# Attention's PSUM banks in three kinds, its fourth head apart, and DVE's part of each task one round later

## The chip, the cores and the metric

The kernel runs on one core of one Trainium2 chip. Its time is the device time of one launch, in microseconds (us); shorter is better. In the profile the engines are PE (TensorE: matmuls and transposes through an identity), PEld (PE's weight loads), DVE (VectorE), ACT (ScalarE), POOL (GpSimd) and SP (SyncE, which here only issues DMAs). Each engine takes its instructions in the order in which the program lists them; a semaphore makes one wait for another.

## The reference

Two layers, each with adaptive normalisation, an attention and a feed-forward part, over 16 batches (B) of 256 tokens (T) of width 128 (D). The change lies in layer 0's attention, 16 heads of width 8:

```python
h = _layernorm(x, axis=-1) * (1 + ca) + sa          # sa, ca, ga per batch, from silu(c) @ wmod
qkv = h @ Wqkv + bqkv
content = einsum('bhid,bhjd->bhij', q, k)
rel = pad(einsum('bhid,rd->bhir', q, rel_emb), one on the left)[..., :L]
attn = softmax((content + rel) / sqrt(8), axis=-1)
out = einsum('bhij,bhjd->bhid', attn, v)
x = x + ga * (out.reshape(B, L, D) @ Wout + bout)
```

After it come a feed-forward of 16 experts (a router picks 4 of them per token), and layer 1: a cumulative-sum attention with phases, and a gated feed-forward with a time shift. These are in both kernels the same.

## The kernel before

Attention is cut into 64 rounds: 16 batches times NR = 4 rounds of four heads. Two batches make a chunk, eight chunks in all. Round n belongs to batch b = n // 4, r = n % 4.

In a round the four heads g = 0 to 3 lie on 32 partitions each (`rows_ = slice(32 * g, 32 * g + 32)`), so that their matmuls use different rows of PE's array. They go through these steps, spread over rounds:

- `scores(n)` (L446): for each head two matmuls of 32 x 128 x 256 into a bank `s`, 128 x 512. Order: the first half of all four heads, then the second half.
- `row_maxima(n, s)` (L466): DVE takes the negated row maximum of each of the four banks. After an odd round, `maxima` gets the upper bits and (on POOL, L472) the rest.
- `with_maxima(pair)` (L477, L482): every second round DVE transposes the maxima of the two rounds before, and SP moves them into `max_rows` with four DMAs.
- `weights(n)` (L491, L501): LAG = 4 rounds later the transposed scores are computed in banks `st`, starting from the negated maximum (one matmul with `takes`, then two of `kx` by `qx`), and ACT takes their exp (L509) into `exp`.
- `values(n, exp)` (L521): one round after that, 16 PE instructions multiply by `v_aug`, which holds v and a column of ones, into a bank `po`; ACT copies it out (L532, L535), POOL adds (L536).

All eight PSUM banks are one pool, `p_m`. Each tile takes the next bank in turn and waits until the tile that had it eight tiles ago has been read.

Beside the rounds run tasks: Python generators that stop at named places, and go on when the round's loop comes to a place of that name (`take_step`). The places of a round, in order: scores and row maxima, "dve" (statistics of the normalisation, L549, L550), weights, values, "mid" and "end" (PE's part), then the copies that are due, "take" (DVE's part: it reads what "end" left in a bank), one load of later weights, "after", "late" (the router's steps). The tasks are

- `project(c)`: normalises chunk c (POOL scales, L555), transposes it (`pln`, L569), makes q and k (`pq` L627, `pk` L633), splits q and k into upper bits and rest (`halves`: `q_high`, `k_high`, L456, rest by L599) and later v (`pv`, L669). It starts in round 8c-12 for chunk c (chunk 1 in round 0).
- `attn_end(b)`: transposes the output (`pot`, L720), divides by the sums (L724, L726), transposes back (`pu`, L732), multiplies by Wout (`py`, L739), and adds to x (`y`, L742, L743, L744).
- `chunk_end(c)`: the second batch's `attn_end`, then layer 0's second normalisation and the router's logits (`pl`, L750, L754).

The operands of scores need each head's four components (upper bits and rest of q and k in all pairings) on neighbouring partitions. So q and k go through DRAM: `put_aside` writes the upper bits and the rest to `q_halves` and `k_halves` (L647, two pairs of DMAs, one pair per round), and `spread` reads the rows for r = 0 to 3 into `qx` and `kx` (L616, a pair per round). `copies` says in which round each pair is issued. Only batch 0's first round goes directly (`at_once`, L592). The tiles `q_whole`, `k_whole`, `q_high`, `k_high` have one buffer each.

Chunk 0 is made ahead of the rounds by `project_first`, batch 0 and then batch 1, with q's DMAs on ACT's queue and k's on SP's.

## Time and profile before

| | us |
|---|---|
| median of 3 runs | 1077.78 (1077.56 to 1080.33) |
| the profiled execution | 1081.92 |
| its span | 1080.1 |
| first maximum of round 0 | 23.71 |
| of round 8 (chunk 1) | 58.48 |
| of round 16 (chunk 2) | 94.31 |
| of round 63, the last | 295.73 |
| first matmul of the experts | 313.34 |

| engine | busy us | share of the span |
|---|---|---|
| PE | 987.2 | 91% |
| DVE | 831.8 | 77% |
| ACT | 703.2 | 65% |
| POOL | 823.2 | 76% |

The granted clock of TensorE was 0.973 of full speed on the mean. "Busy" counts the time in which an engine has an instruction under way; matmuls are pipelined, so a busy PE need not be full. A row of a view names the line, the engine, the operation, the tile written and the tiles read, and the idle time of the engine just before, with what ended it. The first round's times above are starts of L466 in the timeline. The rounds take some 290 of 1080 us; what follows is bound by PE throughout (27.0 of 27.0 us busy in most stretches from 324 us on).

### The profile page before, as it was taken

To read this page: it belongs to the slowest core of one execution; us is meant where nothing else is said; L and a number is where in the kernel's file an instruction comes from. 1 tells how busy PE (TensorE), PEld (TensorE's weight loads), DVE (VectorE), ACT (ScalarE), POOL (GpSimd) and SP (SyncE) were. 2 spreads that over 40 slices of the span, in tenths; PEclk is the share of its full clock that TensorE was granted. 3 is DMA by queue.
4 is the path that set the end of the run, shared out by engine and by line. 5 is a ranking of instruction groups with operands and counts; after the bars stand their busy time and mean duration, and the time that the engine had idled before them with its cause. 6 is when DMAs were issued, how large, how long until landed. Compare 5 with 4: busy or idle time off the path is not lost. (4 is left out here: it accounts for less than half of the span.)

```text
span 1080.1 us, 14265 instructions
## 1 busy us (share of the span) xinstructions
PE 987.2 (91%) x4529; PEld 483.3 (45%) x4529; DVE 831.8 (77%) x1296; ACT 703.2 (65%) x1490; POOL 823.2 (76%) x807
## 2 busy tenths in 40 slices
PE   5778988889999999999999999898999999999987
PEld 4444555456544444444444434333444444444334
DVE  4858888888835465866556555799999999999995
ACT  2446666666675778787867756365767668768662
POOL 2636556554366777888878788899999999999992
PEclk9989989788999999999999999999999999999999
DMA  5654643233042222223322322200000000000000
GB/s 169 217 180 145 204 153 139 88 120 133 7 151 85 98 98 80 107 90 117 108 89 98 99 87 89 78 10 11 10 10 29 11 20 30 0 10 6 5 10 20
DMA packets 58859, 86.74 MB, mean 80 GB/s; under 512 B 13312, under 2 KB 32288, under 8 KB 58784
## 3 DMA queue, kind: packets, MB, share of 16 engines
q1 hardware_dynamic: 55952, 83.47, 22.8%
q10 hardware_dynamic: 2832, 2.36, 0.7%
q8 instruction: 36, 0.59, 0.2%
q14 instruction: 39, 0.32, 0.1%
HBM read 62.73 MB, written 22.29 MB: 79 GB/s over the span
## 5 line engine op out<-in xcount | busy, mean ns | idle before, releaser
L509 ACT ACTIVATE exp<-st 128x512 f32<-128x512 f32 x256 | 132.2, 603 | 89.9 <-PE st L501 89.8
L466 DVE TENSOR_REDUCE raw<-s 128x2 f32<-128x512 f32 x256 | 160.2, 678 | 20.3 <-PE s L446 20.3
L918 POOL TENSOR_TENSOR u<-u,wide 128x512 f32<-128x512 f32 x128 | 162.8, 1272 | 10.3 <-DVE u L917 0.2
L917 DVE SCALAR_TENSOR_TENSOR u<-pg,u 128x512 f32<-128x512 f32 x128 | 87.7, 686 | 78.8 <-POOL u L911 78.7
L926 PE MATMUL acc<-u,w_dn 128*128 128x512 f32 x256 | 133.7, 604 | 6.3 <-POOL u L918 6.1
L1331 DVE TENSOR_TENSOR_SCAN sum_assoc<-keep,bound_assoc 128x1024 f32<-128x1024 bf16 (+1 forms) x58 | 125.8, 2170 | 9.5 <-POOL bound_assoc L1328 9.5
L903 PE MATMUL pg<-hT,w_gu 128*128 128x512 f32 x256 | 131.2, 594 | 0.4 <-DVE logits L754 0.4
L905 PE MATMUL pup<-hT,w_gu 128*128 128x512 f32 x256 | 130.8, 592 | 0.6 <-ACT u L908 0.6
L911 POOL TENSOR_SCALAR u<-u 128x512 f32<-128x512 f32 x128 | 79.4, 620 | 63.0 <-ACT u L908 55.7
L1328 POOL TENSOR_TENSOR bound_assoc<-v,phasor 128x1024 f32<-128x1024 f32 x57 | 124.7, 2187 | 1.7 <-ACT phasor L1314 1.6
L1549 POOL TENSOR_TENSOR sum_assoc<-sum_assoc,phasor 128x1024 f32<-128x1024 f32 (+1 forms) x58 | 121.5, 2095 | 0.6 <-DVE sum_assoc L1331 0.6
L1331 DVE TENSOR_TENSOR_SCAN mem<-keep,bound_pos 128x1024 f32<-128x1024 bf16 x52 | 118.2, 2272 | 0.0
L906 ACT ACTIVATE pg<-pg,b_gu 128x512 f32<-128x512 f32 x128 | 84.0, 656 | 51.8 <-PE pg L903 51.3
L1328 POOL TENSOR_TENSOR bound_pos<-v,rotor 128x1024 f32<-128x1024 f32 x51 | 111.5, 2186 | 0.0
L1345 PE MATMUL pout<-m_pos,w_pos 128*128 128x512 f32 x204 | 97.2, 599 | 14.2 <-ACT oT L1370 10.7
L1345 PE MATMUL pout<-sum_assoc,w_assoc 128*128 128x512 f32 x228 | 107.6, 594 | 2.0 <-POOL sum_assoc L1549 1.8
L908 ACT ACTIVATE u<-pup,b_gu 128x512 f32<-128x512 f32 x128 | 87.8, 686 | 18.4 <-PE pup L905 16.7
L521 PE MATMUL po<-exp,v_aug 128*32 128x256 f32 x1024 | 80.1, 435 | 10.3 <-DVE raw L466 10.0
L1312 ACT ACTIVATE phasor<-off 128x512 f32<-128x512 f32 x56 | 35.1, 627 | 68.8 <-DVE off L1306 67.5
L926 PEld LDWEIGHTS acc<-u,w_dn 128*128 128x128 f32 x256 | 46.6, 189 | 73.8 <-issue 39.0
L905 PEld LDWEIGHTS pup<-hT,w_gu 128*128 128x128 f32 x256 | 50.2, 196 | 60.5 <-issue 51.2
L491 PE MATMUL st<-max_rows,takes 32*128 32x512 f32 x256 | 58.2, 476 | 14.6 <-DVE heads L726 10.2
(313 smaller groups left out, 1869.6 us busy)
## 6 DMA issues: line engine op xcount, KB each, us to landing
wide<-scores SPq DMA_DIRECT2D x64, 512.0 KB, 3.6
qx<-q_halves SPq DMA_DIRECT2D x28, 256.0 KB, 3.1
kx<-k_halves SPq DMA_DIRECT2D x28, 256.0 KB, 3.0
q_halves<-q_high SPq DMA_DIRECT2D x7, 512.0 KB, 3.1
k_halves<-k_high SPq DMA_DIRECT2D x7, 512.0 KB, 3.7
q_halves<-q_whole SPq DMA_DIRECT2D x7, 512.0 KB, 3.1
k_halves<-k_whole SPq DMA_DIRECT2D x7, 512.0 KB, 4.3
there<-total SPq DMA_DIRECT2D x12, 256.0 KB, 2.1
```

What stands on the lines that cost most here:

```text
L466: nc.vector.tensor_reduce(raw[:, :, g, n % 2], s[g], AX.X, ALU.max, negate=True)
L509: nc.scalar.activation(e[:, g, :, :], st[g], AF.Exp, scale=QSCALE)
L903: nc.tensor.matmul(pg, w_gu[:, e, 0 : 2 * D : 2], h2, start=True, stop=True)
L905: nc.tensor.matmul(pu, w_gu[:, e, 1 : 2 * D : 2], h2, start=True, stop=True)
L908: nc.scalar.activation(u, pu, AF.Identity, bias=b_gu[:, 1, e : e + 1])
L917: nc.vector.scalar_tensor_tensor(u, pg, MOST, u, ALU.min, ALU.mult)
L918: nc.gpsimd.tensor_tensor(u, u, wide[n // SOME][:, n % SOME, :], ALU.mult)
L926: nc.tensor.matmul(accs[c], w_dn[:, e, :], work.pop(n), start=False, stop=(e == NE - 1))
L1328: nc.gpsimd.tensor_tensor(w[nm], v2, bind, ALU.mult)
L1331: nc.vector.tensor_tensor_scan(dst[:, half].rearrange("p s k t -> p (s k t)"), keep.rearrange("p (s k) t -> p s k t", k=2)[:, half].rearra ...
L1345: nc.tensor.matmul(pos[c], w[:, j, :], m[:, k, :, :].rearrange("p k t -> p (k t)"), start=(j == 0 and i == 0 and k == 0), stop=(c < NCH - ...
L1549: nc.gpsimd.tensor_tensor(m[:, part], m[:, part], phasor[(n - 1) % 3][:, part, :, 1:], ALU.mult)
```

## The change

- **Banks.** The eight banks become three pools: three for `s`, three for `st`, two for everything else in the rounds. Ahead of the rounds, `bank` goes round a list of the pools.
- **Fourth heads apart.** A round's PE order becomes: the fourth head's `st` of the round before (weights n-5), `s` of heads 0 to 2, `st` of heads 0 to 2 (weights n-4), `s` of head 3, then values, "mid", "end". With three banks each, `s` of head 3 takes head 0's bank of the same round, and `st` of head 2 takes the bank of the fourth head's `st` just before.
- **"take" moves.** DVE's part of a task no longer ends its round; it runs between the maxima of heads 1 and 2 of the next round. q's upper bits, which were taken at "mid", move there too (ahead of k's). The copies that follow from it are counted from that round, so they leave a round later; the wait before `pv` is one shorter.
- **First batches.** The statistics of batches 0 and 1 are taken one after the other, their projections follow each other, `pv` of both comes last. Only the four direct DMAs of batch 0's q stay on ACT's queue; all other moves and reads of chunk 0 are issued by SP, first the eight moves, then the fourteen reads.

```diff
-            p_m = scope.enter_context(tc.tile_pool(name="pa_m", bufs=8, space=bass.MemoryType.PSUM))
+            p_s, p_st, p_m = (
+                scope.enter_context(tc.tile_pool(name=nm, bufs=n, space=bass.MemoryType.PSUM))
+                for nm, n in (("pa_s", 3), ("pa_st", 3), ("pa_m", 2))
+            )
...
-            home = {"psum": p_m}
+            home = {"psum": [p_s, p_s, p_st, p_st, p_m, p_m, p_s, p_st]}
             def bank(shape, nm):
-                return home["psum"].tile(shape, F32, tag="m", name=nm)
+                homes = home["psum"]
+                homes.append(homes.pop(0))
+                return homes[-1].tile(shape, F32, tag="m", name=nm)
...
-            def scores(n):
+            def scores(n, s, heads):
-                s = [bank([P, NIT, T], f"s_{n}_{g}") for g in range(4)]
+                for g in heads:
+                    s[g] = p_s.tile([P, NIT, T], F32, tag="m", name=f"s_{n}_{g}")
                 for i in range(NIT):
-                    for g in range(4):
+                    for g in heads:
...
                     if g == 0 and n >= 2 and n % 2 == 0:
                         with_maxima(n // 2 - 1)
+                    if g == 1:
+                        take_step("take", True)
...
-            def weights(n):
+            def weights(n, heads):
-                st = [bank([P, NIT, T], f"st_{n}_{g}") for g in range(4)]
+                st = {g: p_st.tile([P, NIT, T], F32, tag="m", name=f"st_{n}_{g}") for g in heads}
...
                 nc.scalar.activation(qf, pq, AF.Identity, bias=bq)
-                q = halves(True, qf, nc.gpsimd)
                 yield "end"
...
                 nc.vector.scalar_tensor_tensor(
                     kf, pk, bk, rel.unsqueeze(1).to_broadcast([P, n, T]), ALU.add, ALU.add
                 )
+                q = halves(True, qf, nc.gpsimd)
                 k = halves(False, kf, nc.gpsimd if c else nc.vector)
...
-                    queue = nc.scalar if of_q and not c else nc.sync
                     if not c and not of.start:
-                        at_once(c, of, of_q, parts, 0, queue)
+                        at_once(c, of, of_q, parts, 0, nc.scalar if of_q else nc.sync)
...
                 if not c:
-                    for each in moves + reads[0 if of.start else 1 :]:
-                        for go in each:
-                            go()
+                    firsts.extend(go for each in moves for go in each)
+                    reads_first.extend(go for each in reads[0 if of.start else 1 :] for go in each)
+                    yield "values"
                 for i, each in enumerate(moves + reads if c else []):
                     copies.setdefault(now[0] + 1 + i, []).extend(each)
-                for i in range(LAG if c > 1 else 0):
+                for i in range(LAG - 1 if c > 1 else 0):
                     yield "after"
...
-            start(project_first(0, hT_first), rank=0)
-            take_step("dve")
-            modulation(0, wmod0, sc0, (0, 1), p_m)
+            batches = [project_first(k, hT_first) for k in range(2)]
+            for k in (0, 0, 0):
+                next(batches[k])
+            modulation(0, wmod0, sc0, (0, 1), p_s)
+            for k in (1, 1):
+                next(batches[k])
...
+            for go in firsts + reads_first:
+                go()
+            for k in range(2):
+                assert next(batches[k], None) is None
...
-                    s = scores(n)
+                if n > LAG:
+                    weights(n - LAG - 1, (3,))
+                s = {}
+                if n < len(rounds):
+                    scores(n, s, (0, 1, 2))
+                if LAG <= n < len(rounds) + LAG:
+                    weights(n - LAG, (0, 1, 2))
+                if n < len(rounds):
+                    scores(n, s, (3,))
                     row_maxima(n, s)
...
-                if LAG <= n < len(rounds) + LAG:
-                    es[n - LAG] = weights(n - LAG)
...
-                take_step("take", True)
```

More of the change, by code (lines that the diff above doesn't have):

```diff
@@ L399, in rest_of_setup @@
             def rest_of_setup():
-                modulation(0, wmod0, sc0, (3, 4, 5), p_m)
+                modulation(0, wmod0, sc0, (3, 4, 5), p_st)
                 pg = bank([B, D], "pgate")
@@ L452, in scores @@
                         )
-                return s
             def upper(out, src):
@@ L482, in with_maxima @@
                     nc.sync.dma_start(rows_[m], turned[32 * m : 32 * m + 16])
-            def weights(n):
+            def weights(n, heads):
                 b, r = rounds[n]
                 c, k = divmod(b, 2)
-                e = ap.tile([P, 4, NIT, T], F32, tag="exp", name=f"exp_{n}")
-                st = [bank([P, NIT, T], f"st_{n}_{g}") for g in range(4)]
-                for g in range(4):
+                if n not in es:
+                    es[n] = ap.tile([P, 4, NIT, T], F32, tag="exp", name=f"exp_{n}")
+                st = {g: p_st.tile([P, NIT, T], F32, tag="m", name=f"st_{n}_{g}") for g in heads}
+                for g in heads:
                     rows_ = slice(32 * g, 32 * g + 32)
@@ L498, in weights @@
                 for i in range(NIT):
-                    for g in range(4):
+                    for g in heads:
                         rows_ = slice(32 * g, 32 * g + 32)
@@ L507, in weights @@
                         )
-                for g in range(4):
-                    nc.scalar.activation(e[:, g, :, :], st[g], AF.Exp, scale=QSCALE)
-                return e
+                for g in heads:
+                    nc.scalar.activation(es[n][:, g, :, :], st[g], AF.Exp, scale=QSCALE)
             def values(n, e):
@@ L583, in operands @@
                 )
-            copies, now = {}, [-1]
+            copies, now, firsts, reads_first = {}, [-1], [], []
             def at_once(c, of, of_q, parts, r, queue):
@@ L641, in projected @@
                 for of_q, parts in ((True, q), (False, k)):
-                    queue = nc.scalar if of_q and not c else nc.sync
                     if not c and not of.start:
-                        at_once(c, of, of_q, parts, 0, queue)
-                    both.append((of_q, *put_aside(at, of_q, parts), queue))
-                moves = [
-                    [(lambda queue=queue, move=moves[i]: queue.dma_start(*move)) for _, _, moves, queue in both]
-                    for i in range(2)
-                ]
+                        at_once(c, of, of_q, parts, 0, nc.scalar if of_q else nc.sync)
+                    both.append((of_q, *put_aside(at, of_q, parts)))
+                moves = [[(lambda move=moves[i]: nc.sync.dma_start(*move)) for _, _, moves in both] for i in range(2)]
                 reads = [
-                    [
-                        (lambda r=r, of_q=of_q, there=there, queue=queue: spread(c, of, of_q, there, r, queue))
-                        for of_q, there, _, queue in both
-                    ]
+                    [(lambda r=r, of_q=of_q, there=there: spread(c, of, of_q, there, r)) for of_q, there, _ in both]
                     for r in range(NR)
@@ L657, in projected @@
                 if not c:
-                    for each in moves + reads[0 if of.start else 1 :]:
-                        for go in each:
-                            go()
+                    firsts.extend(go for each in moves for go in each)
+                    reads_first.extend(go for each in reads[0 if of.start else 1 :] for go in each)
+                    yield "values"
                 for i, each in enumerate(moves + reads if c else []):
                     copies.setdefault(now[0] + 1 + i, []).extend(each)
-                for i in range(LAG if c > 1 else 0):
+                for i in range(LAG - 1 if c > 1 else 0):
                     yield "after"
-                yield "mid"
+                if c:
+                    yield "mid"
                 tiles = slice(2 * of.start, 2 * of.stop)
@@ L694, in project_first @@
                 hn = cross.tile([P, NIT, D], F32, tag="hn4", name=f"hn_a0_{k}")
+                yield "tokens"
                 for i in range(NIT):
@@ L698, in project_first @@
                     )
-                for i in range(2 * k):
-                    yield "after"
                 yield "mid"
@@ L791, in tile_adaln_two_layers @@
             hT_first = ap1.tile([P, 2, T], F32, tag="hT", name="hT_0")
-            start(project_first(0, hT_first), rank=0)
-            take_step("dve")
-            modulation(0, wmod0, sc0, (0, 1), p_m)
-            start(rest_of_setup(), rank=2)
-            for place in ("mid", "mid", "end", "take", "mid"):
-                take_step(place)
-            start(project_first(1, hT_first), rank=0)
-            for place in ("dve", "after", "after", "mid", "mid", "end", "take", "mid"):
-                take_step(place)
+            batches = [project_first(k, hT_first) for k in range(2)]
[4 more added lines that the diff above has]
+                next(batches[k])
+            start(rest_of_setup(), rank=2)
+            assert next(batches[0]) == "mid"
+            assert next(batches[1]) == "mid"
+            for place in ("end", "take", "values"):
+                assert next(batches[0]) == place
+            for place in ("mid", "end", "take", "values"):
+                assert next(batches[1]) == place
+            for go in firsts + reads_first:
+                go()
+            for k in range(2):
+                assert next(batches[k], None) is None
             for i in range(2):
@@ L808, in tile_adaln_two_layers @@
             es = {}
+            home["psum"] = [p_m]
             next_chunks = {max(0, 2 * NR * c - 4): c + 1 for c in range(NCH - 1)}
@@ L816, in tile_adaln_two_layers @@
                         start(first_scores(n - (len(rounds) - NR)))
-                    s = scores(n)
+                if n > LAG:
[7 more added lines that the diff above has]
+                    scores(n, s, (3,))
                     row_maxima(n, s)
-                elif n == len(rounds):
-                    with_maxima(n // 2 - 1)
+                else:
+                    if n == len(rounds):
+                        with_maxima(n // 2 - 1)
+                    take_step("take", True)
                 take_step("dve")
-                if LAG <= n < len(rounds) + LAG:
-                    es[n - LAG] = weights(n - LAG)
                 if n >= LAG + 2 and rounds[n - LAG - 2][1] == NR - 1:
@@ L840, in tile_adaln_two_layers @@
                 if n < LAG:
-                    for place in ("mid", "end", "take"):
+                    for place in ("mid", "end"):
                         take_step(place)
@@ L1182, in tile_adaln_two_layers @@
             ready = prepare()
-            home.update(psum=p_m)
+            home.update(psum=[p_m])
             def last_end():
```

## The prediction

> **What bounds the kernel now.** I read the stages first, by the windows of the profiled execution (columns: stretch, its length, busy time and instructions of PE, PEld, DVE, ACT, POOL, then the granted clock, DMA share and GB/s).

> ```profile
> 23.70:58.50 34.80, 23.84 (x186) 13.81 (x190) 25.62 (x64) 13.12 (x28) 18.87 (x31) 0.97 0.70 224
> 58.50:94.30 35.80, 30.03 (x326) 16.93 (x322) 26.59 (x57) 21.07 (x46) 16.73 (x24) 0.84 0.52 166
> 94.30:126.80 32.50, 29.00 (x338) 18.05 (x336) 27.85 (x68) 21.86 (x49) 19.73 (x31) 1.00 0.56 185
> 126.80:161.90 35.10, 30.62 (x338) 18.70 (x337) 28.52 (x66) 22.36 (x49) 19.48 (x30) 0.90 0.49 157
> 313.30:1080.10 766.80, 728.14 (x1832) 325.51 (x1832) 594.60 (x728) 518.66 (x1096) 667.22 (x550) 1.00 0.16 56
> ```

> The change touches only what lies ahead of 313.3; behind it stand 766.8 us that take what they are given. The stretches from 58.5 on are eight rounds each (rounds 8 to 15, 16 to 23, 24 to 31). DVE works 27.9 of 32.5 us in rounds 16 to 23, PE 29.0: neither is full, they wait for each other. Then the waits of 94 to 296 us, DVE's own:

> ```profile
> DVE raw L466 <- PE s L446: 9.3, 15, 1.7
> DVE y L742 <- PE py L739: 9.2, 12, 1.9
> DVE logits L754 <- PE pl L750: 5.2, 6, 1.3
> DVE q_high L456 <- ACT q_whole L629: 3.6, 5, 1.3
> ```

> 27.3 us in 48 rounds, the prize in view. How one round closes, in the timeline (start, length, engine, line, names; in brackets the idle time before), round 19:

> ```profile
> 106.40 0.81 PE L446 MATMUL s<-kx,qx 32*128 32x256 f32 x8
> ...
> 106.94 1.30 PE L491 MATMUL st<-max_rows,takes 32*128 32x512 f32 x4
> ...
> 107.14 2.49 DVE L466 TENSOR_REDUCE raw<-s 128x2 f32<-128x512 f32 x4 [0.36 <-PE s L446]
> ...
> 108.41 1.07 PE L521 MATMUL po<-exp,v_aug 128*32 128x256 f32 x16
> ...
> 109.41 0.66 PE L569 MATMUL pln_f<-ident,hn_f 128*128 128x128 f32 x4
> ...
> 109.90 0.61 PE L739 MATMUL py<-wout,oT 128*128 128x128 f32 x4
> ...
> 110.44 0.51 PE L446 MATMUL s<-kx,qx 32*128 32x256 f32 x8
> 110.55 0.42 DVE L742 TENSOR_TENSOR y<-py,ga 128x256 f32<-128x256 f32 x1 [0.71 <-PE py L739]
> ```

> The round lasts 3.84 us, from the first maximum to the next (110.98). Last the SP queue of the front, where the waits are longest (PE waits 8.1 us for kx there):

> ```profile
> 53.64 0.58 SPq L616 DMA_DIRECT2D qx<-q_halves  x1
> ...
> 59.39 2.48 SPq L482 DMA_DIRECT2D max_rows<-turned  x4
> 61.91 0.99 SPq L616 DMA_DIRECT2D qx<-q_halves  x1
> 62.95 0.43 SPq L616 DMA_DIRECT2D kx<-k_halves  x1
> 63.42 0.64 SPq L135 DMA_DIRECT2D gates<-in_gate_dram  x1
> 64.11 0.62 SPq L616 DMA_DIRECT2D qx<-q_halves  x1
> ```

> These reads fetch chunk 1's rows, one index r per round, two rounds ahead of use. The r=3 pair (64.11) stands behind the second gates load. For kx in this window (64 to 65 us) the view of the tile says

> ```profile
> DMA to landing us min/median/max: 8.9/8.9/8.9
> ```

> where the median of all its reads is 3.0.

> **The change, part by part.** Times are of the first maximum of a round unless said otherwise.

> *First batches.* Batch 1's chain no longer stands behind ACT's queue (its v_aug copy waited 7.83 us), so its pq can start near 14 instead of 20.02. But q_whole, q_high, k_whole have one buffer each. ACT's second q_whole now waits until SP has written batch 0's halves: SP issues 4 first-round DMAs from 11.4 (0.61 each) and 4 moves (0.6 each), to 16.4; a move lands 2.8 to 3.3 us after its issue, so about 18.4 for q and 19.1 for k. DVE then needs 1.6 for batch 1's four operations, SP 2.4 for its four moves, and the first read of round 1's rows leaves at 22.4, landing near 25.5. Behind the waiting q_whole stand ACT's two v_aug copies, which free banks of round 0. Round 0 begins about 20.3 instead of 23.71, but round 1 about 26.6 instead of 27.09. Gain 0.5; ends 3.4 (all that round 0 gains) and a loss of 2.

> *Banks by kind, at the front.* With eight common banks PE computed round 3's scores early and began batch 2's transposes at 32.02, under round 2. With three score banks the fourth head of round 3 waits for that round's own first maximum, so the transposes start near 34.5. They are ready only at 33.5, so about 1 us of the 2.5 is lost: round 4 begins at 41.1 instead of 40.10.

> *DVE's part a round later, at the front.* k_whole, q_high, k_high (1.45 us, from 98.48 to 100.05 less a gap) move into round 4 (3.33 before, 5.0 now with its 0.9 of statistics). Rounds 5 and 6 lose 0.15 and 0.6 to the score banks. Round 6 begins 2.8 late. The two pairs of moves and the four reads all leave one round later; the second pair is now behind round 6's max_rows (2.6 us on SP). From there: landing 3 to 5, reads 1.0, landing 2.9, scores 0.9: round 8 begins at 61.8, 3.3 late (ends 1.5 and 4.5).

> *Reads one round ahead.* Round 9's rows are issued after round 8's max_rows: 0.8+2.5+1.0+2.9+0.2 = 7.4 us, as the 7.58 that this round takes now, covered by pq and pk on the slow clock. Round 10's rows stand behind the second gates load. With the 8.9 us landing its predecessor lasts 7.8 instead of 3.33: 4.5 lost (ends 0, were they to land in 3, and 5.5). Round 11's wait for round 10's max_rows: 7.3 instead of 5.28, 2.0 lost (ends 0 and 3). Chunks 2 to 7 keep four rounds between read and use, so there it costs nothing. Rounds 11 to 15 lose 1 (below). The front: 3.3+4.5+2.0+1.0 = 10.8, ends 2.5 and 14.

> *Rounds 16 to 63.* Two chains bind a round; its length is the longer one. PE's: maximum of head 0 (0.69), restart 0.06, the fourth head's two matmuls (0.23 apart: eight take 0.51, one 0.28), 0.21 to po, 1.00 for po to the next work, the tasks T, then the last round's fourth head of st, 0.35 (take 0.23, from 115.66 to 115.89, and 0.12), then 0.53 from scores to the maximum: 3.07+T, and 0.1 more where st's third bank waits for the exp of the fourth head (0.60) just issued. T until scores: pq and pk 1.92, pot 0.58, pu 0.37, pln and py 1.03, pv and pl 1.89. DVE's: 2.49 for four maxima, 0.16 for a transpose, its takes, 0.93 for maxima and statistics, or, without statistics, 0.48 from the last maximum to the next first: the third score bank frees only then, and such a wait is 0.48 where it shows now (rounds 54, 62).

> - Round 16: PE 3.16+1.92 = 5.05. Round 17: DVE 2.49+1.45+0.93 = 4.9.
> - 18 and 22: DVE 2.49+0.16+0.70 (inv, heads)+0.48 = 3.85 each.
> - 19 and 23: PE 3.16+1.03 = 4.2 each. 20: PE 3.16+1.89 = 5.05. 21: 3.7.

> The sum is 34.8 against 32.5, 2.3 lost per eight rounds at full clock, with DVE's three waits gone: where PE is long DVE idles, where DVE is long PE does, and three banks let no round run ahead. The ends: 1.5 gained (the exp wait and the 0.48 hidden, 0.35 overlapped) and 5 lost (all tasks a second time late). Six stretches: 13 lost, ends -9 and +30. POOL's subtractions (1.27 each) and bias steps follow their DVE step by a round; their readers are three rounds off. SP's max_rows still have two rounds.

> Here the fourth head by itself matters. In the trace four row groups start together (eight scores in 0.51, one lasts 0.28). [...] The rows of this trace charge it 0.35 and 0.44 in rounds that PE sets and nothing in the others.

> *Clock and tail.* Stretches with a half-speed spell last 35.1 against 32.5. The long idle of PE behind one DVE take (1.9 us at most before st) is split in two, so I take 5 us off for six spells (ends -15 and +6). The five rounds after the last scores take 14.8 us (298.5 to 313.3); the exp of a fourth head between takes adds some 0.4 each: 2, ends 0 and 4. [...]

> **Sum.** 10.8+13-5+2 = +20.8 on the profiled execution's 1081.92, which is 4.1 above the median of the three runs; on the median, 1077.78+20 = 1098.

> **The rivals.**
> - *DVE runs through.* If the new bank waits stay under 0.2 us and the heads apart cost PE nothing, the 27.3 us of DVE waits go, 5 come back, and the front loses only 3: 1059. For it: DVE's waits name PE work that is a round old after the change. Against: the 0.48 waits, and PE's 29.0 of 32.5. It decides from a mean round under 3.9 us (now 4.2).
> - *Slow clock.* PE now sets more rounds, so half-speed spells cost more. Rounds 40 to 47, granted 0.81, take 36.6, 4.1 over the 32.5 at full clock (some of it routing). The four stretches from 126.8 to 269.1 exceed 32.5 by 12.3 together; were all six to exceed it by 4.1, 24.6, my -5 becomes +12: 1115.
> - *The loss is hidden.* The front's waits overlap (r=2 lands in 3 us) and the mean round stays 4.2: 1077 to 1084, by the 2.5 of the front.

> **How the numbers follow.** Forecast (1084 to 1112) 0.56, slow clock 0.17, hidden 0.12, half of it within 0.3% (3.2 us, about what a measurement of this kernel can tell from no change), DVE through 0.15. Faster 0.15, same 0.06, slower 0.79. The range, 1078 to 1116, leaves out the faster case and the upper part of the slow clock.

> **What would show it.** Right: round 8 begins near 62, round 10 near 78, round 11 near 85; PE waits for kx rise from 8.1 to some 20 us; waits for py and pl at DVE vanish, while raw waits for s grow in nearly every round; eight rounds at full clock last 34 to 35. Wrong: a mean round under 4.0 us, round 16 before 97, or scores that start without waiting for the maximum of the head before.

## The result, and the profile after

The changed kernel takes 1140.06 us (median of 4 runs, 1136.11 to 1149.22) against 1078.01: a ratio of 1.0583, 95% interval 1.0518 to 1.0648. The forecast was 1098, its range 1078 to 1116. The direction was right, the size was not: +62 us, not +20.

The profiled execution took 1149.22 us, its span is 1147.4. That is 67.3 over the span of before, more than the medians' difference; the executions of the changed kernel differ by 13 us among themselves, and their granted clock on the mean lies between 0.935 and 0.956. By stage, from the starts of first maxima (us):

| | before | after | more | forecast |
|---|---|---|---|---|
| start to round 16 | 94.3 | 110.8 | 16.5 | 10.8 |
| round 16 to round 63 | 201.4 | 240.0 | 38.6 | 13 - 5 |
| round 63 to the end | 784.4 | 796.6 | 12.2 | 2 |

First the windows of the changed kernel (stretch, length, busy time and instructions of PE, PEld, DVE, ACT, POOL, then granted clock, DMA share, GB/s). The first is rounds 8 to 15, the next three are eight rounds each from round 16 on:

```profile
64.06:110.78 46.72, 39.40 (x327) 23.45 (x323) 26.59 (x56) 22.29 (x46) 17.19 (x24) 0.78 0.40 129
110.78:149.78 39.00, 33.09 (x336) 20.48 (x336) 28.72 (x67) 23.64 (x49) 19.31 (x30) 0.87 0.51 160
149.78:194.64 44.86, 38.92 (x336) 24.64 (x336) 28.69 (x66) 23.84 (x49) 19.32 (x30) 0.73 0.38 124
194.64:232.89 38.25, 31.63 (x336) 19.50 (x336) 30.26 (x73) 23.65 (x49) 19.42 (x30) 0.96 0.33 114
```

DVE's work is about what it was (28.7 us in rounds 16 to 23, 27.9 before), but eight rounds last 38 to 45 us, and the clock column is the one that differs most between stretches that hold nearly the same program: 0.73 goes with 44.9 us, 0.96 with 38.2. Added up over all rounds from 16 to 63, the records of the clock hold 81.9 us at half speed, against 37.5 before. In both kernels these are six spells; before, each lasted 3.4 to 6.8 us, now 3.4 to 23.9. The profiled executions are no exceptions: from the mean clock of each run (1.0 and 0.5 are the only values in the records) the whole of the changed kernel had 100 to 148 us at half speed in its four runs, that of the kernel before 24 to 87 in all of its runs.

The waits of rounds 16 to 63 (who waits, for whom: us in all, times, longest):

```profile
DVE raw L471 <- PE st L509: 63.1, 33, 4.7
...
PEld st L499 <- ACT exp L517: 39.1, 48, 3.0
...
PE st L499 <- ACT exp L517: 26.9, 37, 2.7
```

DVE's waits for `py`, `pl` and `q_whole` are gone from this list, as forecast. In their place DVE waits at the first maximum of a round, 63.1 us in 33 waits, where its four kinds of waits came to 27.3 (the profile puts it down to `st`, whose matmuls start together with the scores, at 198.90 and 198.91 in round 33), and PE waits for an exp before the third head of `st`. One round at full clock, round 35, the counterpart of round 19 (both hold `pln` and `py`; it lasts 4.68 us, not 3.84; the forecast for its kind was 4.2):

```profile
210.52 2.49 DVE L471 TENSOR_REDUCE raw<-s 128x2 f32<-128x512 f32 x4 [1.57 <-PE st L509]
211.10 0.50 PE L499 MATMUL st<-max_rows,takes 32*128 32x512 f32 x1 [0.68 <-ACT exp L517]
...
211.77 1.07 PE L528 MATMUL po<-exp,v_aug 128*32 128x256 f32 x16
...
212.77 0.66 PE L576 MATMUL pln_f<-ident,hn_f 128*128 128x128 f32 x4
...
213.72 0.71 PE L739 MATMUL py<-wout,oT 128*128 128x128 f32 x4 [0.29 <-ACT o L539]
...
215.20 0.69 DVE L471 TENSOR_REDUCE raw<-s 128x2 f32<-128x512 f32 x1 [1.98 <-PE st L509]
```

PE stands still 0.68 us before `st`, for ACT's exp, and DVE 1.98 before the next maxima, for PE: the engines wait for each other inside one round. And the SP queue of the front, with the pair of reads that the forecast spoke of behind the second load of the gates:

```profile
68.71 0.65 SPq L135 DMA_DIRECT2D gates<-in_gate_dram  x1
69.40 0.62 SPq L623 DMA_DIRECT2D qx<-q_halves  x1
70.07 0.43 SPq L623 DMA_DIRECT2D kx<-k_halves  x1
```

That pair landed 8.2 us after its issue, and round 9 lasted 7.30 us instead of 3.33.

### The profile page after: what moved, and what is told of

The parts are those of the page before. It is cut to its first block, busy times and chain, and to the rows that moved or that the text cites. A ratio compares the mean times of both kernels' runs of the same rounds, so it can differ in the third digit from the quotient of the medians.

```text
span 1147.4 us, 14224 instructions
## 1 busy us (share of the span) xinstructions
PE 1044.2 (91%) x4529; PEld 520.3 (45%) x4529; DVE 835.3 (73%) x1296; ACT 716.6 (62%) x1492; POOL 822.7 (72%) x807
## 5 line engine op out<-in xcount | busy, mean ns | idle before, releaser
L471 DVE TENSOR_REDUCE raw<-s 128x2 f32<-128x512 f32 x256 | 164.6, 680 | 100.2 <-PE st L509 72.2
L517 ACT ACTIVATE exp<-st 128x512 f32<-128x512 f32 x256 | 139.1, 598 | 107.9 <-PE st L509 70.6
L499 PE MATMUL st<-max_rows,takes 32*128 32x512 f32 x256 | 93.7, 532 | 34.3 <-ACT exp L517 34.1
L1361 PE MATMUL pout<-m_pos,w_pos 128*128 128x512 f32 x204 | 99.8, 612 | 12.7 <-ACT oT L1386 9.9
L452 PE MATMUL s<-kx,qx 32*128 32x256 f32 x512 | 89.5, 397 | 22.3 <-DVE raw L471 10.9
L528 PE MATMUL po<-exp,v_aug 128*32 128x256 f32 x1024 | 90.1, 479 | 0.1
L509 PE MATMUL st<-qx,kx 32*128 32x256 f32 x512 | 82.9, 346 | 0.0
```

Source lines behind the costliest of these rows:

```text
L471: nc.vector.tensor_reduce(raw[:, :, g, n % 2], s[g], AX.X, ALU.max, negate=True)
L499: nc.tensor.matmul(st[g], takes[rows_, n % 2, :], max_rows[n // 2 % 3][rows_, :].unsqueeze(1).to_broadcast([32, NIT, T]), start=True, stop ...
L517: nc.scalar.activation(es[n][:, g, :, :], st[g], AF.Exp, scale=QSCALE)
L528: nc.tensor.matmul(po[32 * g : 32 * g + 32, :], v_cols[:, 2 * k + i, at + 64 * g : at + 64 * g + 32], e[:, g, i, :], start=(i == 0), stop= ...
L1361: nc.tensor.matmul(pos[c], w[:, j, :], m[:, k, :, :].rearrange("p k t -> p (k t)"), start=(j == 0 and i == 0 and k == 0), stop=(c < NCH - ...
```

## The experiments

Every time below is a median, with the ratio to the kernel before and its 95% interval. "Half speed" is the time at a granted clock of 0.5 in the profiled execution, one for each kernel, between the first maxima of rounds 16 and 63 unless said otherwise. The expectations count more: their 118 us for the changed kernel and 54.6 for the kernel before hold the front and the last rounds too. "Port" is my word there for a DVE instruction that lasts longer while POOL works (1.16 us instead of 0.18); what the two share no run shows.

### Each part alone

**Banks by kind and fourth heads apart.** The kernel before with the three pools, the new `scores(n, s, heads)` and `weights(n, heads)`, and this order:

```diff
+                if n > LAG:
+                    weights(n - LAG - 1, (3,))
+                s = {}
+                if n < len(rounds):
+                    scores(n, s, (0, 1, 2))
+                if LAG <= n < len(rounds) + LAG:
+                    weights(n - LAG, (0, 1, 2))
+                if n < len(rounds):
+                    scores(n, s, (3,))
                     row_maxima(n, s)
```

> The kernel before with only the three kinds of banks and the fourth heads apart; DVE's part of a task stays at the end of its own round, the first batches as before. Theory (half clock): the wait of PE for the exp of the fourth head (0.68 us a round in the changed kernel) stands in each half-speed stretch and keeps the clock from rising, so half-speed time grows from 54.6 us to 80 or more, and the kernel takes 1100 to 1120. Rival (pattern at full clock): three banks cost about 2 us per eight rounds and nothing else, half-speed time stays near 55: 1088 to 1096. Rival (the moved step alone does it): 1075 to 1085.

Measured: 1135.34 us, 1.0513 (1.0463 to 1.0563). Most of the loss is here, more than either theory allowed. Half speed is 54.6 us where 37.5 stood, so the clock has a share, but eight rounds at full clock also last longer. The window of its rounds 24 to 31:

```profile
140.57:175.71 35.14, 29.06 (x336) 18.11 (x336) 27.83 (x67) 23.32 (x49) 19.37 (x31) 1.00 0.48 149
```

35.1 us against the 32.5 of before, with PE busy 29.1 and DVE 27.8: the same work, further apart. From round 16 to 63 that kernel takes 228.4 us (27.0 more), to round 16 it takes 105.5 (11.2 more), behind round 63 796.8 (12.4 more). Of the 11.2, 6.0 are there at round 0, which begins at 29.75 instead of 23.71; the changed kernel, with the first batches, begins it at 20.53.

**DVE's part a round later.**

```diff
+                    if g == 1:
+                        take_step("take", True)
...
-                q = halves(True, qf, nc.gpsimd)
                 yield "end"
...
+                q = halves(True, qf, nc.gpsimd)
                 k = halves(False, kf, nc.gpsimd if c else nc.vector)
...
-                take_step("take", True)
```

> The kernel before with only DVE's part of a task moved between the maxima of heads 1 and 2 of the next round (q's upper bits with it, copies a round later); eight common banks, heads together, first batches as before. Theory (port): in the rounds that take k's part the upper bits of the maxima last 1.15 us instead of 0.18, because POOL subtracts at that moment; about 5 us in all, and DVE's 23 us of waits for py, pl and q_whole mostly go, as eight banks let PE run ahead: 1065 to 1085. Rival (the moved step is the loss by itself): 1095 or more, with PE waiting for DVE's raw behind the step.

Measured: 1103.66 us, 1.0224 (1.0209 to 1.024): the rival. DVE is busy 173.8 us from round 16 to 63, 170.2 before and 173.5 in the changed kernel, where the upper bits of the maxima last 1.16 us in four of these rounds; no gain stands against it. Half of the loss is in the front (round 16 at 105.35 instead of 94.31: 6.7 us in rounds 9 and 10, whose rows come late, and 2.5 already at round 0), half in the rounds (212.3 against 201.4, at the same 37.5 us of half speed).

**First batches.** The kernel before with the change's `project_first`, its order of first steps, and SyncE's moves.

> The kernel before with only the first batches normalised one after the other and SyncE moving chunk 0's rows. By the prediction's step round 0 begins 3.4 us earlier, round 1 0.5 earlier, and the gain ends there: 1074 to 1080. Rival (SyncE's moves hold up the reads of rounds 1 to 4): round 4 begins 1 to 3 us later, 1079 to 1084.

Measured: 1076.47 us, 0.9968 (0.9948 to 0.9988). Round 0 starts at 20.14 instead of 23.71, round 1 at 25.92 instead of 27.09, round 4 at 38.94 instead of 40.10. A small gain, its interval just clear of 1.

**Fourth heads apart, eight common banks.** As the first experiment, but `p_s` and `p_st` are `p_m`.

> The kernel before with only the fourth heads apart, in PE's new order, but all eight banks common; DVE's part and first batches as before. Theory (the three kinds of banks make the loss of the banks alone, 1135): no bank is waited for, eight rounds at full clock last 32.5 to 33.5, half-speed time near 55: 1079 to 1090. Rival (the fourth head apart makes it, by its own take and products, whatever the banks): 1115 to 1135, eight rounds at 35.

Measured: 1078.17 us, 0.9987 (0.9959 to 1.0014). With eight common banks the head apart costs nothing in all. The trace of the changed kernel shows part of the reason (timeline, start of round 33):

```profile
198.90 0.50 PE L499 MATMUL st<-max_rows,takes 32*128 32x512 f32 x1
...
198.91 0.50 PE L452 MATMUL s<-kx,qx 32*128 32x256 f32 x6
```

The fourth head of `st` and heads 0 to 2 of `s` stand next to each other in PE's order and lie on different rows of the array: they start together (198.90 and 198.91). `st` of heads 0 to 2 and `s` of head 3 are neighbours in PE's order too. The head is not free where PE sets a round: the first maximum waits for `st` too.

```profile
199.73 1.29 DVE L471 TENSOR_REDUCE raw<-s 128x2 f32<-128x512 f32 x2 [1.33 <-PE st L509]
```

It starts 0.82 us after the scores (198.91). In the kernel before this is 0.53 where the scores of all four heads start together (115.32 to 115.85 in round 21). The prediction put 0.53 and 0.35, 0.88 in all.

### The banks, by kind

**All eight common in the changed kernel:**

```diff
-            p_s, p_st, p_m = (
...
+            p_m = scope.enter_context(tc.tile_pool(name="pa_m", bufs=8, space=bass.MemoryType.PSUM))
+            p_s = p_st = p_m
```

> The changed kernel with all eight banks common again; fourth heads apart, the moved step and the first batches as in the change. By the parts measured alone (moved step +24, fourth heads apart with common banks -1, first batches -3) 1095 to 1103 if they add up; the part of the banks in the changed kernel is then 37 to 45 of its 62 us. If the banks matter only where they are alone (banks alone gave +56): 1120 or more.

Measured: 1098.92 us, 1.0179 (1.0141 to 1.0217). The other three parts add up, and the kinds of banks are worth 1140.1 - 1098.9 = 41 of the 62 us. Taken alone from the kernel before they cost 56, so with the banks among them the parts do not simply add.

**Three banks for scores, five common; and three for the transposed scores, five common:**

```diff
-                for nm, n in (("pa_s", 3), ("pa_st", 3), ("pa_m", 2))
+                for nm, n in (("pa_s", 3), ("pa_m", 5))
...
+            p_st = p_m
```

The second edit is the same with `p_st` and `p_s` exchanged.

> The changed kernel with two kinds of banks: three for scores alone as in the change, the other five common to the transposed scores and all else. The exp wait of PE is gone by this, the wait of the fourth head for its round's first maximum stays. Theory A (the scores' three banks tie PE to DVE's maxima, and PE, which can't work ahead, loses its clock): 1125 or more, half-speed time over 90. Theory B (the transposed scores' three banks do it, by the exp wait): 1095 to 1110, near the moved step alone (1104).

> The changed kernel with two kinds of banks the other way round: three for the transposed scores alone, five common to scores and all else. The exp wait (0.68 us a round) stays, scores may run ahead of the maxima by two banks more. Theory A (the scores' three banks): 1095 to 1110, half-speed time under 80. Theory B (the transposed scores' three banks): 1125 or more, PE waits for exp of 40 us or more.

Measured: 1119.79 us, 1.0373 (1.0329 to 1.0416), and 1118.99 us, 1.0375 (1.0322 to 1.0428). Neither theory: each kind is about half of it, 20 us over the common banks. One takes away the scores' head start (PE's scores wait 27.9 us for DVE's maxima in rounds 16 to 63, 2.4 with common banks), the other makes PE wait for the exp before `st` (29.2, none with common banks). Half speed is 44.4 us in both and 47.8 with common banks, so the clock does not explain these 20 us.

### POOL's subtraction and DVE's upper bits

In five of the rounds of the changed kernel that take k's part (9, 17, 25, 33 and 49) one small instruction of DVE lasts six times as long as elsewhere, a collision with POOL. DVE and POOL in round 33 of the changed kernel:

```profile
203.76 1.16 DVE L461 TENSOR_SCALAR maxima<-raw 128x16 int32<-128x16 int32 x1
```

```profile
203.62 1.27 POOL L606 TENSOR_TENSOR k_whole<-k_whole,k_high 128x512 f32<-128x512 f32 x1
```

Elsewhere it takes 0.18 us (0.41 in round 41); here it ends when POOL's subtraction does (204.9). The edit issues that subtraction right behind the round's maxima:

```diff
-                k = halves(False, kf, nc.gpsimd if c else nc.vector)
+                k = halves(False, kf, None if c else nc.vector)
...
+                if c:
+                    yield "rest"
+                    nc.gpsimd.tensor_tensor(k[1], k[1], k[0], ALU.subtract)
...
+                take_step("rest")
                 take_step("dve")
```

> The changed kernel, but POOL's subtraction of k's upper bits is issued behind the maxima of the same round, so it no longer runs while DVE takes the upper bits of the maxima. Theory (port and clock together): that instruction falls from 1.16 to 0.18 us in the five rounds that show it, PE's idle behind those rounds falls from 1.6 to about 0.6 us, most of the 3.4 us stretches in which PE is busy under 0.6 go, half-speed time falls from 118 to under 90: 1110 to 1125. Rival (the port costs only itself): 5 us, half-speed time unchanged: 1132 to 1137. Rival (POOL's turn is no cause): the instruction stays at 1.16 and the time at 1140.

Measured: 1143.69 us, 1.0604 (1.0586 to 1.0621). The instruction is back at its 0.18 us, with the subtraction now behind it (round 25, DVE and POOL):

```profile
160.20 0.18 DVE L461 TENSOR_SCALAR maxima<-raw 128x16 int32<-128x16 int32 x1
```

```profile
160.64 1.27 POOL L664 TENSOR_TENSOR k_whole<-k_whole,k_high 128x512 f32<-128x512 f32 x1
```

So the cause of the 1.16 is shown; the time is not mended, and lies outside all three ranges. Rounds 24 to 31 of that kernel, which met no half speed:

```profile
151.07:185.95 34.88, 30.50 (x336) 19.12 (x336) 27.65 (x67) 23.47 (x49) 19.30 (x30) 1.00 0.50 158
```

34.88 us, where the forecast's sum said 34.8. Rounds 16 to 63 fell from 240.0 to 225.1, with 47.8 us of half speed instead of 81.9. But half speed up to round 16 rose from 20.5 to 51.2 us, round 16 came at 114.84 instead of 110.78, and the median stayed (the profiled execution of this kernel was its fastest, that of the changed kernel its slowest). The pair of measurements, 1.16 us beside POOL's subtraction and 0.18 us ahead of it, is what the runs show of the collision.

### The clock

```profile
203.36:206.77 3.41, 1.57 (x16) 1.05 (x16) 3.31 (x9) 2.15 (x4) 2.62 (x5) 1.00 0.00 0
206.78:210.19 3.41, 3.41 (x30) 1.81 (x29) 2.14 (x5) 0.74 (x2) 2.38 (x4) 0.50 0.06 10
```

PE is busy for 1.57 of 3.41 us while DVE finishes k's part and the late maxima, and the next step is granted 0.50. The records of this kernel show eight drops to half speed up to 376 us: in the step ahead of seven PE was busy 0.72 to 2.16 us, ahead of one 2.64. It is no sharp limit: in the kernel before a step with 2.01 (from 49.77 us) was followed by full speed.

**The fourth head of `st` right after values.** I took the 0.68 us wait for the exp as what keeps the clock down once it has fallen, and moved that head so that its exp is over long before:

```diff
-                if n > LAG:
-                    weights(n - LAG - 1, (3,))
...
                     values(n - LAG - 1, es.pop(n - LAG - 1))
+                if LAG <= n < len(rounds) + LAG:
+                    weights(n - LAG, (3,))
```

> The changed kernel, but the fourth head's transposed scores follow values in their own round instead of opening the next, so its exp is over long before the third head needs that bank. Theory (the exp wait keeps the clock down): the waits of PE for exp go from 66 us (with weight loads) to under 15, half-speed time falls from 118 to under 60, and the kernel takes 1095 to 1115. Rival (PE's wait for DVE keeps it down): half-speed time stays over 90 and the time over 1125.

Measured: 1240.02 us (four runs, 1213 to 1245, all with a mean clock of 0.83 to 0.86; even the fastest is 64 us above the slowest of the changed kernel). My theory fell: PE's waits before `st` for the exp went from 26.9 to 0.7 us (its weight loads, which run beside its matmuls, 35.41 us of them within 56.82 busy us of PE below, still wait 35.4), and half speed went up to 305.8 us. Eight rounds with half speed throughout, 40 to 47:

```profile
261.10:317.92 56.82, 56.82 (x339) 35.41 (x339) 33.63 (x81) 24.41 (x48) 20.18 (x32) 0.50 0.23 76
```

56.8 us for eight rounds. PE is busy all the time in the records and the clock does not come back, so "busy" there is not what brings it back.

**With both edits.**

> The changed kernel with both edits: POOL's subtraction of k's upper bits behind the maxima, and the fourth head's transposed scores right after values. Theory: both triggers of half speed are gone in rounds 16 to 63, which take 6 times 34.9 us (rounds 24 to 31 with the subtraction moved) and some routing, 214 to 220 instead of 240; the front stays 12 to 18 late: 1095 to 1112. Rival (half speed comes back elsewhere, as it did with the subtraction alone): 1120 or more.

Measured: 1212.88 us (1186 to 1228), half speed 266.2 us: the rival, worse than foreseen.

**Idle matmuls.** Four matmuls a round that compute nothing (the filler), in the bank that values then overwrite:

```diff
+                if n > LAG:
+                    po = bank([P, T], f"po_{n - LAG - 1}")
+                    for i in range(FILLS):
+                        nc.tensor.matmul(po[:, 0:P], ident, ident, start=True, stop=True)
                 if LAG <= n < len(rounds) + LAG:
                     weights(n - LAG, (0, 1, 2))
```

> The changed kernel with four more matmuls (identity by identity, 128 x 128, into the bank that values then overwrite) ahead of the transposed scores of heads 0 to 2, where PE waits 0.68 us for the fourth head's exp: nothing is computed with them. Theory (activity of PE sets the clock): the stretches of 3.4 us at half speed are then full, the clock rises after one or two, half-speed time falls from 118 to under 70, and the kernel with more work takes 1105 to 1125. Rival (the clock is no cause but a consequence): 65 rounds by up to 0.66 us more, 1150 to 1185.

Measured: 1133.33 us, 1.0492 (1.0453 to 1.0532), 7 below the changed kernel with 256 matmuls more (the slowest run, 1135.35, is below the fastest there, 1136.11; the intervals overlap). It lies between the ranges of theory and rival. Half speed is 10.2 us instead of 81.9. The gain is small because the matmuls are on the path: rounds 24 to 31 at full clock

```profile
147.46:186.33 38.87, 37.66 (x401) 25.80 (x402) 28.62 (x66) 23.20 (x49) 19.32 (x30) 1.00 0.43 138
```

last 38.9, where the same with neither filler nor POOL's collision lasts 34.9. The edit also claims the bank of `po` earlier; that by itself was not tried.

**The same filler with the moved head** (ahead of the scores of head 3):

> The changed kernel with the fourth head's transposed scores right after values (1240 alone, 306 us of half speed in rounds 16 to 63), and four idle matmuls a round (identity by identity, 128 x 128, into the bank that values overwrite) ahead of the scores of head 3. Theory (too little activity of PE holds it at half speed, and that is what the 100 us more are): half-speed time in the rounds falls under 80 us and the time to 1120 to 1160, with more work. Rival (the place of the fourth head is slow by itself): 1200 or more.

Measured: 1155.14 us, 1.0707 (1.0665 to 1.0749), down from 1240 with more work. No half speed at all in the rounds:

```profile
165.28:206.35 41.07, 40.81 (x403) 29.06 (x400) 28.69 (x66) 24.19 (x49) 19.27 (x30) 1.00 0.41 131
```

Eight rounds last 41.1 instead of 56.8 us. So most of the 1240 was the clock; the order with its filler is some 2 us in eight rounds dearer than the changed kernel's with its own (41.1 against 38.9). With the filler the clock did not fall in these rounds (1.00 on the mean over their 240.01 us), but the filler does not always bring it back: ahead of round 16 the same kernel stayed at half speed for 30.7 us in one piece, with the idle matmuls in every round and PE busy throughout:

```profile
86.47:117.18 30.71, 30.71 (x180) 21.26 (x177) 12.96 (x31) 9.79 (x19) 7.61 (x13) 0.50 0.26 84
```

**Filler and freed subtraction**, two and four matmuls:

> The changed kernel with POOL's subtraction behind the maxima and two idle matmuls a round in PE's wait for the fourth head's exp. Theory (the half clock is what is left beside the pattern and the port): eight rounds last 35 to 36, little half speed in the rounds, 1110 to 1122, 18 or more below the changed kernel. Rival (two matmuls are too few, or the clock is a consequence only): half-speed time of 48 us and more in the rounds, 1130 to 1145 as with the subtraction alone (1144).

> The same with four idle matmuls. Theory: no half speed in rounds 16 to 63, eight rounds of 37.9 (38.9 with the wait filled, less 1.0 for the subtraction): 1124 to 1132, dearer than two if two suffice. Rival: as with the wait filled alone, 1133 or more.

Measured: 1121.43 us, 1.0395 (1.0367 to 1.0423), and 1127.72 us, 1.0454 (1.0426 to 1.0482). With two, half speed in the rounds is 27.3 us and the kernel is 22 us faster than with the subtraction alone (1143.69): half speed is not only a consequence of slow rounds. The time lies at the upper end of the theory's range. With four it is 0.0, as that theory said, and the rounds take 223.5.

### The two parts that cost nothing, together

The kernel before with the change's first batches and its fourth heads apart; eight common banks, DVE's part where it was.

> The kernel before with the first batches of the change and its fourth heads apart, eight common banks, DVE's part at the end of its own round: the two parts that cost nothing alone. Alone they gave -3.2 and -0.9 us: 1071 to 1077 if they add up, 1079 if the earlier first round is lost again.

Measured: 1073.04 us, 0.9949 (0.9928 to 0.9969): 5.9 us faster than before, faster than both kernels.

## Why the prediction was wrong in size

Point by point, on the profiled executions (67.3 us more, 20.8 forecast).

- **First batches**, forecast 0.5 gained at round 1: 1.2 in the kernel that has this alone, and the total fell by 3.2. Right within its ends.
- **The front**, forecast 10.8: 16.5. The steps came near where they were put: round 4 at 41.94 (41.1), round 8 at 64.06 (61.8), round 10 at 79.17 (78), round 11 at 87.30 (85). The pair behind the second load of the gates landed late by about the amount taken (8.2 us, 8.9 forecast). PE's waits for `kx` came to 8.7 us (8.1 before), not 20; with 1.5 for `qx` they are 10.2. Of the 5.7 us missed 2.3 are there at round 8; most of the rest is "rounds 11 to 15 lose 1": they took 23.5 us instead of 19.6, with half speed in them up to 97.6.
- **Rounds 16 to 63 at full clock**, 34.8 us in eight forecast: 34.88 measured where neither the clock nor POOL interferes. The two chains of the sum hold, round by round (3.16+1.92 is 5.08, which the prediction wrote as 5.05): 5.08 for round 24 (forecast of its kind 5.05), 4.95 for 25 (4.9), 3.78 for 26 (3.85), 4.25 for 27 (4.2), 5.02 for 28 (5.05), 3.68 for 29 (3.7), 3.82 for 30 (3.85), 4.30 for 31 (4.2).
- **POOL's subtractions**, which the prediction set aside with "their readers are three rounds off": their readers are, but DVE's next instruction was not looked at. Four full collisions and a small one lengthen DVE's instruction by 4.2 us in rounds 16 to 63. With four idle matmuls and no half speed, rounds 24 to 31 last 38.87 with the collision and 37.90 without, so it lies on the path in full.
- **The clock**, the step that failed. The prediction wrote "The long idle of PE behind one DVE take (1.9 us at most before st) is split in two, so I take 5 us off for six spells". That shorter idle of PE means less half speed was my estimate; no run shows the 5 us. The stall was not split: with three banks for scores, PE stands still while DVE does k's part and the two maxima behind it, and the stretch of 1.57 busy us is the result. The spells were six, as put, but not shorter: half speed went from 37.5 to 81.9 us in the rounds. Its price, an estimate: rounds 16 to 63 take 223.5 us with four filler matmuls, no half speed and no collision; the filler costs 37.9 - 34.9 = 3.0 in eight rounds, 18 in six times eight; so 205.5 at full clock. 240.0 - 205.5 - 4.2 leaves 30 us for 81.9 us of half speed. For the kernel before, the kernel with only the first batches gives a rate: 201.4 - 194.1 = 7.3 us less at 37.5 - 13.7 = 23.8 less half speed, 0.31 per us, so 12 us for its 37.5. The difference is 18 us lost where 5 gained were put, and the full-clock part comes out at 205.5 - 190 = 16 (13 forecast). A second estimate: the kernel with the subtraction moved takes 225.1 us in these rounds with 47.8 of half speed, so, less the 4.2, 10.7 us go with 34.1 of half speed, 0.31 per us again. By that rate the 81.9 cost 26 us and the loss is 14.
- **The tail**, forecast 2: 12.2. It is lost before the last exp (27.2 us from round 63's first maximum to its start, 14.4 before); from there on both take 769 to 770 us. Two things changed in that stretch. Half speed went from 3.4 to 17.1 us. And ACT changes its table back and forth, as it does with the banks alone and with the wait filled, but not with two kinds of banks or with common ones. ACT of the changed kernel, in the timeline:

```profile
355.01 1.28 ACT L922 ACT_TABLE_LOAD   x1
356.30 0.66 ACT L922 ACTIVATE pg<-pg,b_gu 128x512 f32<-128x512 f32 x1
356.98 1.28 ACT L517 ACT_TABLE_LOAD   x1
358.28 1.58 ACT L517 ACTIVATE exp<-st 128x512 f32<-128x512 f32 x3
```

The first expert's gate now stands among the last exps in ACT's program; before, it stood behind all of them (one load, at 312.45). It seems that the gate's banks are free once the scores' own three are, so it is placed there; that is argued from the order of the program, no run tried it. The tail with the waits filled, which met no half speed before its last exp, is 791.9 us: 7.5 more than before for the loads and the exp waits, which leaves some 5 for the clock.
- **The fourth head apart**: the rows charged it 0.35 and 0.44 us in the rounds that PE sets. In the changed kernel's rows it is 0.29 where the first maximum waits for PE (0.82 against 0.53), near the 0.35; with eight common banks it cost nothing in all (0.9987). Apart from its own round's heads it still has neighbours in PE's order with which it starts together (198.90 and 198.91 in round 33).
- **The rivals.** "Slow clock" named the right cause and a price (1115) that was too low, because it priced only spells like those of before. "DVE runs through" was wrong: DVE's waits rose from 27.3 to over 63 us. So was "the loss is hidden": the mean round went from 4.3 to 5.1 us, and the front lost 16.5.

By these estimates the clock is 14 to 18 us in the rounds and some 7 in front and tail, against -5 put: 26 to 30 of the 46 us missed; the rest is the tail's order, the collisions, the front and 3 to 7 us of the pattern at full clock. What stays open is what the granted clock follows. It changes on a grid of 3.41 us; it fell behind a stretch with PE busy 1.57 of 3.41 us, and it did not rise in stretches that the records show busy throughout (56.82 of 56.82). With idle matmuls of 128 x 128 it stayed up in rounds 16 to 63 (0.0 us of half speed with four of them and the subtraction moved), but 30.71 busy us with them among the rest did not raise it.

## What to carry to other kernels

Banks kept apart by kind take away an engine's right to run ahead. What that cost at full clock (2.4 us in 32.5 here, 16 in the rounds by the estimate) was about half of the loss in the rounds; the clock, whose spells of half speed lasted up to 23.9 us instead of 6.8, was nearly as much or more. Price a change of waits with the clock that the new gaps will be granted, stretch by stretch, and look for what else runs on POOL at the moment to which a DVE instruction is moved (1.16 us instead of 0.18 here). Measure the parts of a change alone: here two of four were a gain together (0.9949) and were hidden by the others.

## What the runs showed of the hardware that was not expected

- Idle matmuls made kernels faster: 1240 to 1155 us with four more a round (fastest runs 1213 and 1151), 1144 to 1121 with two.
- The half clock held with PE busy in every record: in the kernel with the head moved for 56.82 us in one piece, eight rounds that take about 35 at full clock in the changed order. From round 16 to 63 it was 305.8 of 326.2 us there.
- A DVE instruction on 128 x 16 elements took 1.16 us instead of 0.18 while POOL subtracted 128 x 512.
